# A planned attention and FFN kernel: new transfer prices and new priorities for its planner

## The chip, the cores and the metric

The kernel runs on one core of one Trainium2 chip. A core has five engines that run on their own: TensorE (PE: matrix products, written into PSUM), VectorE (DVE: elementwise work and reductions), ScalarE (ACT: activations and copies), GpSimd (POOL: elementwise work), and SyncE (SP), which in this kernel issues every transfer to the 16 DMA engines. Each engine runs its own list of instructions in the order in which the program holds them; semaphores make it wait for the others. The metric is the time of one execution on the device in microseconds (us); lower is better.

## What the kernel computes

A transformer layer on 32 batches of a 128 x 512 tile, with a second 128 x 512 tile per batch as context: cross attention, then a feed-forward network (FFN) with ternary weights and 8-bit activations. Cut to what matters:

```python
x = x + xattn(layernorm(x), ctx)         # 8 heads of 16 channels, 512 queries, 512 keys, rotary
                                         # embedding on 8 of the 16, softmax in float32
x = x + ffn(layernorm(x))

def ffn(x):
    gate = act_quant(x) @ weight_quant(w_gate).T      # 512 -> 2048
    up = act_quant(x) @ weight_quant(w_up).T
    return act_quant(fwht(silu(gate) * up)) @ weight_quant(w_down).T   # 2048 -> 512
# act_quant: per row, scaled by its largest magnitude to whole numbers of -128..127
# weight_quant: to -1, 0, 1 by the mean magnitude of the whole matrix
# fwht: Walsh-Hadamard transform over the 2048 columns
```

## The kernel before

**The stages.** The work is cut into stages, each a Python generator (`s_load`, `s_a`, ..., `s_dn`) that goes through the batches b = 0 to 31, or through the 64 units u (half a batch, four heads, each). For one batch they do this:

- Load x and ctx (`s_load`), normalise (`s_a`), project queries and keys (`s_a2`, PE lines 556 and 557, in groups of 32 columns), rotate them (`s_a3`, POOL), split each number in two parts for the faster float32 format and write all to a DRAM buffer `xd` (lines 620 to 674). Four transfers a unit (`s_st`, lines 695 and 697) read it back head by head into `qs` and `ks`, of which there are four each.
- Scores once for the row maximum: `s_mpe` (PE line 726, a pair of matmuls on 48 rows into `pS`), `s_mdve` (DVE line 741). `s_mfin` transposes the maxima (PE line 763), and sends them by way of DRAM (`md`, lines 772 and 777) into two spare rows of `qs`.
- Scores again, transposed and with the maximum taken off: `s_epe` (PE line 796, a pair of matmuls on 50 rows into `pT`); the exponent `s_eact` (ACT line 809); the product with the values `s_eav` (PE line 830, `pav`, in groups of 32 columns, with the sum of the exponents beside it).
- `s_u` copies `pav` out and stores it (line 872). `s_o` reads sums, values and x back (lines 913 to 922), inverts the sums, spreads the inverse by way of DRAM (`rd`, `RB`, lines 930 and 935), multiplies, and projects (PE line 948). The last batch alone takes a path with fewer transfers.
- `s_o2` normalises and quantises; the gates and ups follow (`s_gpe`, `s_upe`, PE line 1013, in chunks of four matmuls; ACT line 1043; DVE line 1068), the Walsh-Hadamard transform (`s_bf`, line 1097 on POOL or DVE, then transposes on PE line 1117 and products on lines 1156 and 1157), the quantisation (`s_am` to `s_q2`), and the last product (`s_dn`, PE lines 1274 and 1275) with the store of the result (line 1284).

Ahead of and beside the first batches `s_w` loads the three weight matrices in twelve 1 MB tiles (line 438), and `s_w1` to `s_w4` find their scale and round them (ACT lines 451, 475, 493; DVE line 485; POOL line 477). The first gate waits until all twelve are rounded. PSUM has one buffer each for `pS`, `pT` and `pav` and three small ones, `pf`, for all the rest.

**The planner.** The order of the instructions is not written out. When the program is built, `Plan.run` goes through a list of the stages. A stage yields what it wants next: an engine and an estimated duration (`"pe", 0.234, "half"`), a transfer (`"dma", 0.73`), a free buffer (`"get"`) or an event of another stage (`"on"`). The planner keeps a clock for each engine, finds which request could start first, and among those that could start on the same engine within `eps` (`epspe` on PE) of it takes the one with the lowest rank. The rank is the stage's entry in `CFG` plus `T` times the batch number; entries ending in `.h` hold for the first four batches and those in `.z` for the last four. `stick` favours PE requests in the array shape that PE is in (`MODE`: full, half, cols), and `TURN` is what the planner counts for a change of shape. Where two engines could do a step, `pen` counts against the second.

A transfer's request has up to three numbers. The first is the time for which it takes the DMA engines, the second the time that SP takes to issue it (0.45 if left out), the third is added to the 2.0 us that the planner counts for its landing. The planner runs these numbers only while building; on the chip nothing but the resulting order is left, and each engine waits where its operands are not ready.

Of the kernel before, what the change touches and what calls it, by code (L numbers as in the profile page):

```python
# [22 lines left out]


CFG = {
    "a": 17204.8,
    "a.h": 56888.9,
    "a.z": 14936.6,
    "a2": 4110.6,
    "a2.h": 10733.7,  # L30
    "a2.z": 4091.9,
    "a3": -1064.4,
    "a3.h": 4876.9,
    "a3.z": 2422.1,
    "am": 4773.1,
    "am.h": 13803.0,
    "am.z": -44218.1,
    "bf": 3144.9,
    "bf.h": 24712.8,
    "bf.z": 19590.3,  # L40
    "const": 14934.4,
    "const.h": 15491.8,
    "const.z": 4076.0,
    "dn": 4293.7,
    "dn.h": 4871.1,
    "dn.z": 21179.4,
    "eact": -36632.4,
    "eact.h": -37814.4,
    "eact.z": -1863.9,
    "eav": 11135.5,  # L50
    "eav.h": 4223.8,
    "eav.z": 32251.8,
    "epe": -40145.6,
    "epe.h": -40187.6,
    "epe.z": -39869.7,
    "gact": 23899.5,
    "gact.h": -26090.9,
    "gact.z": -36563.3,
    "gpe": 56880.8,
    "gpe.h": 18311.9,  # L60
    "gpe.z": 6005.8,
    "hi": -25784.5,
    "hi.h": -26246.1,
    "hi.z": 4960.2,
    "hm": -21491.6,
    "hm.h": -24541.6,
    "hm.z": -28755.2,
    "init": -37791.2,
    "init.h": -23577.8,
    "init.z": -24582.5,  # L70
    "lo": 1897.6,
    "lo.h": 4758.2,
    "lo.z": -37078.3,
    "load": 23789.4,
    "load.h": 4770.3,
    "load.z": -31350.6,
    "mdve": 1736.2,
    "mdve.h": 4251.6,
    "mdve.z": -25448.7,
    "mfin": -25604.8,  # L80
    "mfin.h": 4075.5,
    "mfin.z": 6355.4,
    "mpe": -26070.7,
    "mpe.h": -37503.9,
    "mpe.z": -21599.3,
    "o": -25785.8,
    "o.h": 35362.7,
    "o.z": -786.3,
    "o2": -37005.1,
    "o2.h": -41684.7,  # L90
    "o2.z": -24211.2,
    "q": 13848.2,
    "q.h": -39189.8,
    "q.z": 4318.1,
    "q1": 11956.7,
    "q1.h": 4753.0,
    "q1.z": 21160.0,
    "q2": 1023.0,
    "q2.h": -21667.4,
    "q2.z": -23754.1,  # L100
    "st": -47909.0,
    "st.h": -35889.1,
    "st.z": 21989.2,
    "u": 26418.5,
    "u.h": 5310.5,
    "u.z": 24337.0,
    "udve": 18718.4,
    "udve.h": 12493.6,
    "udve.z": -34405.8,
    "upe": 29615.8,  # L110
    "upe.h": 19928.1,
    "upe.z": 14589.9,
    "v": 27752.8,
    "v.h": 57650.1,
    "v.z": 53459.6,
    "w": 35469.7,
    "w.h": -19469.2,
    "w.z": 18308.4,
    "w1": 24353.6,
    "w1.h": 18083.3,  # L120
    "w1.z": -34718.8,
    "w2": 28388.6,
    "w2.h": 5547.9,
    "w2.z": 12473.5,
    "w3": 31248.0,
    "w3.h": 19526.9,
    "w3.z": 3962.9,
    "w4": 25647.7,
    "w4.h": 6555.5,
    "w4.z": 20517.4,  # L130
    "yv": -26156.9,
    "yv.h": 11959.1,
    "yv.z": 33180.6,
    "zt": 13824.7,
    "zt.h": 15480.3,
    "zt.z": -26679.3,
    "T": 5.6,
    "eps": 0.019,
    "pen": 9.6,
    "stick": 4685.6,  # L140
    "epspe": 0.21,
}

RINGS = {
# [158 lines left out]
def xattn_ffn(  # L303
# [13 lines left out]
    NB, C, T = x.shape  # L317
    NI = wgt.shape[1] // 128

    const = ctx.enter_context(tc.tile_pool(name="const", bufs=1))  # L320
# [60 lines left out]
    p = Plan(nc, RINGS, CFG)  # L381
    p.head = 4
    p.tail = NB - 4
    st = [dict() for _ in range(NB)]
# [46 lines left out]
    def s_w():  # L431
        for n in range(12):
            m, k = divmod(n, 4)
            src = srcs[m][0][k]
            yield "get", WR[n % 4]
            yield "dma", 2.9
            w = fp.tile([128, 2048], F32, name=WR[n % 4], bufs=2 if WR[n % 4] == "z0" else 1)
            nc.sync.dma_start(out=w.rearrange("p (j i) -> p j i", j=4) if m == 2 else w, in_=src)
            WT[n] = w
            p.marks["w", n] = p.done  # L440
            p.now = p.done - 2.9

    def s_w1():
        for m in range(3):
# [93 lines left out]
    def s_load():  # L538
        for b in range(NB):
            s = st[b]  # L540
            yield "at", b
            yield "get", "xt"
            yield "get", "ct"
            yield "get", "cv"
            yield "dma", 0.73
            s["x"] = xp.tile([128, T], F32, name="xt")
            nc.sync.dma_start(out=s["x"], in_=x[b])
            yield "dma", 0.73
            s["c"] = xp.tile([128, T], F32, name="ct")
            nc.sync.dma_start(out=s["c"], in_=cx[b])  # L550
            p.marks["ld", b] = p.done
# [22 lines left out]
    def s_a2():  # L574
        for b in range(NB):
            s = st[b]
            yield "at", b
            yield "on", "ln", b
            ct, ln = s["c"], s["ln"]
            if b == 0:  # L580
                yield "on", "cw"
            yield "get", "R"
            yield "get", "pf"
            yield "pe", 0.98, "cols"
            pr = ps_f.tile([128, 512], F32, name="pf")
            proj(pr, 0, ct, ln)
            yield "act", 0.585
            R = rp.tile([128, T], F32, name="R")
            nc.scalar.activation(R, pr, AF.Identity, bias=BRP[:, 0:1])
            p.put("pf")  # L590
            yield "get", "RR"
            yield "dma", 0.4, 0.56, -0.9
            RR = rp.tile([128, T], F32, name="RR")
            nc.sync.dma_start(out=RR[0:64, :], in_=R[64:128, :])
            yield "dma", 0.4, 0.56, -0.9
            nc.sync.dma_start(out=RR[64:128, :], in_=R[0:64, :])
            p.marks["rr", b] = p.done
            yield "get", "X"
            yield "get", "pf"
            yield "pe", 0.98, "cols"  # L600
            pq = ps_f.tile([128, 512], F32, name="pf")
            proj(pq, 1, ct, ln)
            p.put("ln")
            p.put("ct")
            yield "act", 0.585
            X = rp.tile([128, 4, T], FR, name="X")
            nc.scalar.activation(X[:, 1, :], pq, AF.Identity, bias=BRP[:, 1:2])
            yield "dve", 0.66
            nc.vector.scalar_tensor_tensor(
                X[:, 3, :], pq, BRP[:, 1:2], X[:, 1, :].bitcast(F32), ALU.add, ALU.subtract  # L610
            )
            p.put("pf")
            yield "get", "xd"
            p.mark("a2", b)
            s["R"] = R, RR, X
            xd = s["xd"] = dr.tile([8, 128, T], FR, name="xd")
            xf = X.bitcast(F32)
            xo = xd.bitcast(F32).rearrange("c p f -> p c f")
            yield "dma", 1.6, 0.45
            nc.sync.dma_start(out=xo[:, 1:4:2], in_=xf[:, 1:4:2])  # L620
            yield "dma", 1.6, 0.45
            nc.sync.dma_start(out=xo[:, 5:8:2], in_=xf[:, 1:2].to_broadcast([128, 2, T]))

    def s_v():
# [23 lines left out]
    def s_a3():  # L648
        for b in range(NB):
# [18 lines left out]
            yield "pool", 1.24  # L668
            nc.gpsimd.tensor_tensor(X[:, 2, :], R, X[:, 0, :].bitcast(F32), ALU.subtract)
            p.put("R")  # L670
            yield "dma", 1.6, 0.45
            nc.sync.dma_start(out=xo[:, 0:4:2], in_=xf[:, 0:4:2])
            yield "dma", 1.6, 0.45
            nc.sync.dma_start(out=xo[:, 4:8:2], in_=xf[:, 0:1].to_broadcast([128, 2, T]))
            p.now = p.done
            p.put("X")
# [166 lines left out]
    def s_u():  # L843
        for u in range(NU):
# [23 lines left out]
            U = op.tile([128, T], F32, name="U", bufs=2)  # L868
            nc.scalar.copy(U, TQ.pop(u))
            p.put("pa")  # L870
            yield "dma", 0.73, 0.45, 0.7
            nc.sync.dma_start(out=st[b]["ud"][hf], in_=U)
            p.now = p.done
            p.put("U")
# [11 lines left out]
    def s_o():  # L886
        for b in range(NB):
# [1 line left out]
            yield "at", b  # L889
            yield "get", "xr"  # L890
            if b in SHORT:
                yield "dma", 0.73, 0.45, 1.2
                xr = op.tile([128, T], F32, name="xr")
                nc.sync.dma_start(out=xr, in_=x[b])
                p.marks["xr", b] = p.done
# [12 lines left out]
                continue  # L908
            yield "on", "ud", 2 * b + 1
            ud = s["ud"].rearrange("g (p r) f -> (g p) r f", r=32)  # L910
            yield "dma", 0.1, 0.45, 0.6
            sc = sm.tile([128, 32], F32, name="sc")
            nc.sync.dma_start(out=sc, in_=ud[:, 16, :].rearrange("h (c f) -> h c f", f=32))
            p.marks["sc", b] = p.done
            yield "get", "N"
            yield "dma", 0.73, 0.45, 1.2
            N = op.tile([128, T], F32, name="N")
            nc.sync.dma_start(out=N, in_=ud[:, 0:16])
            p.marks["N", b] = p.done
            yield "dma", 0.73, 0.45, 1.2  # L920
            xr = op.tile([128, T], F32, name="xr")
            nc.sync.dma_start(out=xr, in_=x[b])
            p.marks["xr", b] = p.done
# [1 line left out]
            yield "dve", 0.3  # L925
            rc = sm.tile([128, 32], F32, name="rc")
            nc.vector.reciprocal(rc, sc)
            yield "dma", 0.1, 0.45, -1.0
            rd = dr.tile([8, T], F32, name="rd")
            nc.sync.dma_start(out=rd.rearrange("h (c f) -> (h c) f", f=32), in_=rc)  # L930
            p.now = p.done
            yield "get", "RB"
            yield "dma", 0.73, 0.45, 0.5
            RB = op.tile([128, T], F32, name="RB")
            nc.sync.dma_start(out=RB, in_=rd[:, None, :].to_broadcast([8, 16, T]))
            p.now = p.done
# [323 lines left out]
    def s_dn():  # L1260
        for b in range(NB):
# [18 lines left out]
            nc.vector.scalar_tensor_tensor(ot, ps, s["yc"], s["x1"], ALU.mult, ALU.add)  # L1280
            p.put("pf")
            p.put("x1")
            yield "dma", 0.73
            nc.sync.dma_start(out=out[b], in_=ot)
            p.now = p.done
            p.put("ot")
# [67 lines left out]
```

## Time and profile before

| | |
|---|---|
| median of three runs | 1439.01 us (1437.60 to 1448.16) |
| the profiled execution | 1444.41 us, span of its instructions 1442.5 us |
| PE busy | 1353.4 us, 94% of the span |
| DVE, ACT, POOL busy | 1179.0, 1189.0, 994.7 us |
| mean granted PE clock | 0.950 |
| moved by DMA | 214.15 MB |

The profile comes from one execution. Its page gives busy times; the span in 40 slices of 36 us, where a digit is the busy share in tenths and PEclk the clock that PE was granted, in tenths of full speed; and the chain of work that ended last, followed back from the last instruction. Beside the page the trace answers for any window: busy times, who waited for whom, and a timeline of the instructions. A matmul's end is modelled, so for PE the distances from start to start say what a group takes. L726 stands for line 726 of the kernel.

### The profile page before, as it was taken

What the parts mean: (1) busy time and instruction counts of PE and PEld (TensorE: products, weight loads), DVE (VectorE), ACT (ScalarE), POOL (GpSimd) and SP (SyncE); (2) the same over time, 40 slices, a digit from 0 to 9 for tenths busy, and PEclk for the clock granted to TensorE, in tenths of its full rate; (3) what the DMA queues carried; (4) which work ended last, traced back from release to release, by engine and by line L of the source; (5) the groups of instructions that cost most, each with busy time, mean ns of one, the idle gap of its engine ahead of it and who ended that gap; (6) DMA issues with size and microseconds to landing.
All of it is one profiled execution on the core that took longest, in us unless ns stands there. A gap on an engine that the chain in (4) does not pass through costs nothing.

```text
span 1442.5 us, 21845 instructions
## 1 busy us (share of the span) xinstructions
PE 1353.4 (94%) x7454; PEld 529.8 (37%) x7454; DVE 1179.0 (82%) x1759; ACT 1189.0 (82%) x1574; POOL 994.7 (69%) x781
## 2 busy tenths in 40 slices
PE   3788899999999999999999999999999999999875
PEld 2222233433334333333333344333333343433332
DVE  2875878888898889888888888888888888886784
ACT  5688978888888888888888888888888888889643
POOL 3122229977777777887777787887777788769550
PEclk7596899999999999999999999999999999999986
DMA  8967555555445555555545555555554554321000
GB/s 285 282 201 245 158 159 160 151 152 143 134 147 163 171 171 174 161 153 148 136 134 154 171 167 175 168 162 156 137 141 140 161 166 153 95 65 49 21 15 15
DMA packets 136315, 214.15 MB, mean 148 GB/s; under 512 B 36746, under 2 KB 38924, under 8 KB 135180
## 3 DMA queue, kind: packets, MB, share of 16 engines
q1 hardware_dynamic: 136204, 212.75, 49.7%
q8 instruction: 59, 0.97, 0.3%
q14 instruction: 52, 0.43, 0.1%
HBM read 106.94 MB, written 93.31 MB: 139 GB/s over the span
## 4 chain that ended last, share of the span: by engine, by line
PE 84%; DVE 7%; ACT 4%; DMA 2%; issue 2%; POOL 0%; SPq 0%; ACTq 0%; DVEq 0%; POOLq 0%
PE pav L830 17%; PE pf L1013 15%; PE pT L796 14%; PE pS L726 10%; PE pf L1274 8%; PE pf L1117 4%; PE pf L556 4%; PE pf L1156 3%; ACT P L809 2%; DVE M L741 2%; PE pf L1157 2%; PE pf L948 2%; PE pf L636 2%; DVE ya L1184 1%; PE pf L1275 1%
## 5 line engine op out<-in xcount | busy, mean ns | idle before, releaser
L741 DVE TENSOR_REDUCE M<-pS 128x2 f32<-128x1024 f32 x488 | 595.0, 1219 | 105.0 <-PE pS L726 103.1
L1097 POOL TENSOR_TENSOR z<-z 128x512 f32<-128x512 f32 x491 | 619.0, 1283 | 68.5 <-DVE z L1068 48.5
L809 ACT ACTIVATE P<-pT 128x1024 f32<-128x1024 f32 x512 | 523.2, 1022 | 148.2 <-PE pT L796 146.4
L830 PE MATMUL pav<-P,va 128*32 128x512 f32 x2048 | 283.6, 625 | 0.0
L796 PE MATMUL pT<-qs,ks 50*128 50x512 f32 x1024 | 259.0, 500 | 17.1 <-ACT P L809 16.5
L726 PE MATMUL pS<-ks,qs 48*128 48x512 f32 x976 | 227.2, 458 | 14.8 <-DVE M L741 9.9
L796 PEld LDWEIGHTS pT<-qs,ks 50*128 50x128 f32 x1024 | 98.1, 188 | 240.3 <-ACT P L809 149.9
L1232 POOL TENSOR_TENSOR y<-y,YB 128x1024 f32<-128x1024 f32 x60 | 140.9, 2369 | 34.9 <-ACT YB L1218 34.9
L1013 PEld LDWEIGHTS <-xqT 128*128 128x128 bf16 x1024 | 91.8, 100 | 155.7 <-issue 84.8
L726 PEld LDWEIGHTS pS<-ks,qs 48*128 48x128 f32 x976 | 95.3, 190 | 117.8 <-issue 39.6
L532 POOL TENSOR_TENSOR arstd<-arstd,MHALF 128x1 f32<-128x1 f32 x32 | 18.6, 580 | 170.4 <-DVE arstd L529 134.8
L1013 PE MATMUL pf<-WGQ,xqT 128*128 128x512 fp8e4 x512 | 133.4, 386 | 1.0 <-ACT z L1043 0.6
L1274 PE MATMUL pf<-WDQ,yq 128*128 128x512 fp8e4 x512 | 125.4, 389 | 8.6 <-ACT yq L1256 8.5
L1184 DVE TENSOR_REDUCE ya<-y 128x128 f32<-128x1024 f32 x64 | 127.1, 1986 | 6.6 <-ACT y L1171 6.3
L1013 PE MATMUL pf<-WUQ,xqT 128*128 128x512 fp8e4 x512 | 127.0, 381 | 0.1
L1068 DVE TENSOR_TENSOR z<-z,pf 128x512 f32<-128x512 f32 x128 | 84.6, 675 | 12.9 <-PE pf L1013 8.7
L1140 DVE TENSOR_TENSOR lo<-pf,hi 128x512 fp32r<-128x512 f32 x128 | 85.7, 675 | 6.0 <-ACT hi L1129 5.9
L1043 ACT ACTIVATE z<-pf,tk 128x512 f32<-128x512 f32 x128 | 83.7, 685 | 7.4 <-PE pf L1013 4.7
L1129 ACT CAST hi<-pf 128x512 fp32r<-128x512 f32 x128 | 74.6, 588 | 17.9 <-PE pf L1117 17.9
L1171 ACT COPY y<-pf 128x512 f32<-128x512 f32 x128 | 71.9, 585 | 13.6 <-PE pf L1157 13.3
L1117 PE MATMUL pf<-CM,z 128*128 128x128 f32 x512 | 82.0, 286 | 0.0
L1274 PEld LDWEIGHTS <-yq 128*128 128x128 bf16 x512 | 46.1, 99 | 89.7 <-ACT yq L1256 22.5
(129 smaller groups left out, 1791.5 us busy)
## 6 DMA issues: line engine op xcount, KB each, us to landing
xd<-X SPq DMA_DIRECT2D x128, 512.0 KB
qs<-xd SPq DMA_DIRECT2D x128, 192.0 KB
ks<-xd SPq DMA_DIRECT2D x128, 192.0 KB
ud<-U SPq DMA_DIRECT2D x62, 256.0 KB
xt<-x SPq DMA_DIRECT2D x32, 256.0 KB
ct<-cx SPq DMA_DIRECT2D x32, 256.0 KB
RR<-R SPq DMA_DIRECT2D x64, 128.0 KB
xr<-x SPq DMA_DIRECT2D x32, 256.0 KB
```

Source lines behind the costliest of these rows:

```text
L726: nc.tensor.matmul(ps[e], qs[w, t, bass.ts(qt, 128)], ks[w, t, :], start=True, stop=True)
L741: nc.vector.tensor_reduce(m, ps[2], AX.X, ALU.max)
L796: nc.tensor.matmul(ps[:, e], ks[w, t, bass.ts(kt, 128)], qs[w, t, :], start=True, stop=True)
L809: nc.scalar.activation(P, TQ[u, n], AF.Exp, scale=0.25)
L830: nc.tensor.matmul(av[32 * h : 32 * h + 32, :], va[:, kt, 4 * hf + h, :], P[:, e], start=(kt == 0), stop=(kt == 3),)
L1013: nc.tensor.matmul(ps, xqT[:, k, :], W[:, k, bass.ts(c, 512)], start=(k == 0), stop=(k == 3))
L1097: E[p.eng].tensor_tensor(ix(dv, k), ix(av, 0), ix(av, 1), o)
L1117: nc.tensor.transpose(ps[:, i, :], st[b]["z"][:, bass.ts(4 * c + i, 128)], EYE)
L1140: nc.vector.tensor_tensor(t, F.pop(("z", b, c)), F["hi", b, c].bitcast(F32), ALU.subtract)
L1184: nc.vector.tensor_reduce(ya[:, h], s["y"][:, 8 * h : 8 * h + 8].rearrange("p j t -> p t j"), AX.X, ALU.max, apply_absolute_value=True,)
L1232: E[p.eng].tensor_tensor(y, y, st[b]["YB"].to_broadcast([128, 8, 128]), ALU.mult)
L1274: nc.tensor.matmul(ps, s["yq"][:, j, :], WDQ[:, j, :], start=(j == 0), stop=False)
```

## The change

All of it is in one file. All 116 numbers of `CFG` are new, most durations that the stages yield for their transfers are new, and so are the issue times that several of them give. No stage, buffer, tile or operation is written differently.

```diff
@@ CFG (116 numbers; a few)
-    "a": 17204.8,
+    "a": -2532.0,
...
-    "load": 23789.4,
+    "load": -575.3,
...
-    "mpe": -26070.7,
+    "mpe": -33425.7,
...
-    "st": -47909.0,
+    "st": 28842.6,
...
-    "w": 35469.7,
+    "w": 393.7,
...
-    "T": 5.6,
-    "eps": 0.019,
-    "pen": 9.6,
-    "stick": 4685.6,
-    "epspe": 0.21,
+    "T": 395.9,
+    "eps": 0.0,
+    "pen": 43.6,
+    "stick": 6870.1,
+    "epspe": 0.193,
@@ s_w (1 MB weight tiles)
-            yield "dma", 2.9
+            yield "dma", 3.5
...
-            p.now = p.done - 2.9
+            p.now = p.done - 3.5
@@ s_load (x and ctx, 256 KB each; twice)
-            yield "dma", 0.73
+            yield "dma", 0.85
@@ s_a2, s_a3 (xd, 512 KB; four times)
-            yield "dma", 1.6, 0.45
+            yield "dma", 1.7, 0.9
@@ s_u (ud)
-            yield "dma", 0.73, 0.45, 0.7
+            yield "dma", 0.85, 0.78, 0.5
@@ s_o (xr, N; sc; rd; RB)
-                yield "dma", 0.73, 0.45, 1.2
+                yield "dma", 0.85, 0.87, 0.8
...
-            yield "dma", 0.1, 0.45, 0.6
+            yield "dma", 0.1, 0.87, 0.4
...
-            yield "dma", 0.1, 0.45, -1.0
+            yield "dma", 0.1, 0.6, -1.0
...
-            yield "dma", 0.73, 0.45, 0.5
+            yield "dma", 0.85, 0.87, 0.3
@@ s_dn (the result)
-            yield "dma", 0.73
+            yield "dma", 0.85, 1.1
```

The requests of `s_a2` for RR, of `s_st` and of `s_mfin` keep their numbers.

More of the change, by code (lines that the diff above doesn't have):

```diff
@@ L25 @@
 CFG = {
-    "a": 17204.8,
[L27 to L70, printed above, removed]
@@ L71 @@
-    "lo": 1897.6,
-    "lo.h": 4758.2,
-    "lo.z": -37078.3,
-    "load": 23789.4,
[L75 to L82, printed above, removed]
-    "mpe": -26070.7,
[L84 to L100, printed above, removed]
-    "st": -47909.0,
[L102 to L115, printed above, removed]
-    "w": 35469.7,
-    "w.h": -19469.2,
@@ L118 @@
[L118 to L136, printed above, removed]
-    "T": 5.6,
-    "eps": 0.019,
-    "pen": 9.6,
-    "stick": 4685.6,
-    "epspe": 0.21,
+    "a": -2532.0,
@@ new lines @@
+    "a.h": 33114.6,
+    "a.z": 27998.7,
+    "a2": 7377.7,
+    "a2.h": 9550.0,
+    "a2.z": 11659.5,
+    "a3": 4485.4,
+    "a3.h": -31571.8,
+    "a3.z": -27238.6,
+    "am": -35754.3,
+    "am.h": 27060.1,
+    "am.z": -29871.3,
+    "bf": 28865.4,
+    "bf.h": 10013.1,
+    "bf.z": 6047.4,
+    "const": 27383.4,
+    "const.h": 1044.9,
+    "const.z": 28332.4,
+    "dn": 695.5,
+    "dn.h": -1820.7,
+    "dn.z": 34268.3,
+    "eact": -36926.7,
+    "eact.h": -29576.8,
+    "eact.z": 2200.1,
@@ new lines @@
+    "eav": -502.3,
+    "eav.h": -26459.5,
+    "eav.z": 29410.1,
+    "epe": -40069.7,
+    "epe.h": -41664.0,
+    "epe.z": -32415.8,
+    "gact": -28753.8,
+    "gact.h": 188.3,
+    "gact.z": 12518.5,
+    "gpe": 30872.5,
+    "gpe.h": 548.0,
+    "gpe.z": 14332.3,
+    "hi": -45433.7,
+    "hi.h": 7766.8,
+    "hi.z": 2154.2,
+    "hm": -22913.0,
+    "hm.h": -30776.5,
+    "hm.z": -37316.5,
+    "init": -36934.8,
+    "init.h": 3168.2,
+    "init.z": 11528.9,
+    "lo": 6013.5,
+    "lo.h": 10999.9,
@@ new lines @@
+    "lo.z": -1596.8,
+    "load": -575.3,
+    "load.h": 12329.4,
+    "load.z": 25505.8,
+    "mdve": -6376.4,
+    "mdve.h": -1628.8,
+    "mdve.z": -31523.9,
+    "mfin": -26748.6,
+    "mfin.h": -907.1,
+    "mfin.z": -26027.5,
+    "mpe": -33425.7,
+    "mpe.h": -44727.0,
+    "mpe.z": -27983.0,
+    "o": -25809.9,
+    "o.h": 2935.5,
+    "o.z": -2753.2,
+    "o2": 25667.8,
+    "o2.h": 1574.0,
+    "o2.z": -27401.5,
+    "q": -3567.6,
+    "q.h": 9521.6,
+    "q.z": -29988.5,
+    "q1": 38339.1,
@@ new lines @@
+    "q1.h": 6950.1,
+    "q1.z": -2784.1,
+    "q2": 32562.8,
+    "q2.h": 10947.1,
+    "q2.z": -24556.7,
+    "st": 28842.6,
+    "st.h": 6443.7,
+    "st.z": -30677.7,
+    "u": 3488.2,
+    "u.h": -25790.7,
+    "u.z": 6857.9,
+    "udve": -3394.6,
+    "udve.h": -25455.1,
+    "udve.z": -26412.7,
+    "upe": 9702.2,
+    "upe.h": 35717.0,
+    "upe.z": 12049.9,
+    "v": 28439.3,
+    "v.h": 153.5,
+    "v.z": 31376.8,
+    "w": 393.7,
+    "w.h": 5204.3,
+    "w.z": 3146.7,
+    "w1": 28102.8,
@@ L142 @@
+    "w1.h": -30405.4,
+    "w1.z": -30179.8,
+    "w2": -18406.1,
+    "w2.h": -27297.2,
+    "w2.z": 6384.2,
+    "w3": 599.0,
+    "w3.h": -24520.0,
+    "w3.z": -30777.7,
+    "w4": 32687.6,
+    "w4.h": 5911.8,
+    "w4.z": -36352.1,
+    "yv": 34240.4,
+    "yv.h": -3147.1,
+    "yv.z": -8859.8,
+    "zt": 2587.3,
+    "zt.h": 13194.4,
+    "zt.z": 615.7,
+    "T": 395.9,
[3 more added lines that the diff above has]
+    "epspe": 0.193,
 }
@@ L544, in s_load @@
             yield "get", "cv"
-            yield "dma", 0.73
+            yield "dma", 0.85
             s["x"] = xp.tile([128, T], F32, name="xt")
             nc.sync.dma_start(out=s["x"], in_=x[b])
-            yield "dma", 0.73
+            yield "dma", 0.85
             s["c"] = xp.tile([128, T], F32, name="ct")
@@ L618, in s_a2 @@
             xo = xd.bitcast(F32).rearrange("c p f -> p c f")
-            yield "dma", 1.6, 0.45
+            yield "dma", 1.7, 0.9
             nc.sync.dma_start(out=xo[:, 1:4:2], in_=xf[:, 1:4:2])
-            yield "dma", 1.6, 0.45
+            yield "dma", 1.7, 0.9
             nc.sync.dma_start(out=xo[:, 5:8:2], in_=xf[:, 1:2].to_broadcast([128, 2, T]))
@@ L670, in s_a3 @@
             p.put("R")
-            yield "dma", 1.6, 0.45
+            yield "dma", 1.7, 0.9
             nc.sync.dma_start(out=xo[:, 0:4:2], in_=xf[:, 0:4:2])
-            yield "dma", 1.6, 0.45
+            yield "dma", 1.7, 0.9
             nc.sync.dma_start(out=xo[:, 4:8:2], in_=xf[:, 0:1].to_broadcast([128, 2, T]))
@@ L915, in s_o @@
             yield "get", "N"
-            yield "dma", 0.73, 0.45, 1.2
+            yield "dma", 0.85, 0.87, 0.8
             N = op.tile([128, T], F32, name="N")
@@ L919, in s_o @@
             p.marks["N", b] = p.done
-            yield "dma", 0.73, 0.45, 1.2
+            yield "dma", 0.85, 0.87, 0.8
             xr = op.tile([128, T], F32, name="xr")
@@ L1282, in s_dn @@
             p.put("x1")
-            yield "dma", 0.73
+            yield "dma", 0.85, 1.1
             nc.sync.dma_start(out=out[b], in_=ot)
```

## The prediction

> **What bounds the kernel now.** I read the page's busy table and slices first, then the granted clock beside them, then the chain, then stretches by stage, and last the waits inside the steady part.
>
> ```profile
> PE 1353.4 (94%) x7454; PEld 529.8 (37%) x7454; DVE 1179.0 (82%) x1759; ACT 1189.0 (82%) x1574; POOL 994.7 (69%) x781
> ...
> PE   3788899999999999999999999999999999999875
> ...
> PEclk7596899999999999999999999999999999999986
> DMA  8967555555445555555545555555554554321000
> ...
> PE 84%; DVE 7%; ACT 4%; DMA 2%; issue 2%; POOL 0%; SPq 0%; ACTq 0%; DVEq 0%; POOLq 0%
> ```
>
> TensorE (PE) is 94% busy and holds 84% of the chain. It is not full in the first six slices and in the last three; the DMA engines are near full only in the first two. The stretches make this exact:
>
> ```profile
> 0.00:216.00 216.00, 163.51 (x752) 57.60 (x756) 142.92 (x221) 167.94 (x199) 55.19 (x53) 0.76 0.71 222
> 216.00:340.00 124.00, 122.76 (x715) 47.74 (x711) 105.58 (x157) 104.67 (x142) 108.83 (x87) 1.00 0.51 150
> 340.00:380.12 40.12, 40.12 (x236) 15.84 (x240) 35.15 (x53) 34.82 (x48) 31.98 (x26) 1.00 0.55 157
> 380.12:420.24 40.12, 40.12 (x238) 15.82 (x240) 35.16 (x53) 34.83 (x48) 32.00 (x26) 1.00 0.52 157
> 420.24:1344.00 923.76, 920.17 (x5265) 363.09 (x5263) 793.53 (x1174) 797.51 (x1073) 735.35 (x572) 1.00 0.50 145
> 1344.00:1443.00 99.00, 66.72 (x272) 29.68 (x268) 66.66 (x106) 49.19 (x69) 31.33 (x22) 0.78 0.04 13
> ```
>
> Columns: window, length, busy time (and count) of PE, weight loads, DVE, ACT, POOL, then granted clock, DMA share, GB/s. From about 216 to 1344 us PE is busy all the time at full clock, and one batch takes 40.12 us; DVE (35.2) and ACT (34.8) have 5 us to spare, POOL 8. The ramp leaves PE idle for 52.5 us at a mean clock of 0.76, the tail for 32.3 us. In the steady part the waits are these:
>
> ```profile
> ACT P L809 <- PE pT L796: 89.0, 120, 1.7
> POOL arstd L532 <- DVE arstd L529: 82.9, 14, 6.1
> PEld pT L796 <- ACT P L809: 77.5, 137, 0.9
> ...
> POOL arstd L532 <- DMA RB<-rd: 29.5, 5, 5.9
> ```
>
> (Engine and line that waited, what it waited for, total us, times, longest, over 340 to 1140 us.) The only sizeable wait there for a transfer is POOL's, which has 8 us a batch to spare; PE has none. So **better prices of transfers have nothing to win in the 1100 us where the batch period is made**. What the change can do there is alter the order of PE's own work, for better or worse.
>
> **The change, part by part.** Same work: counting the two built programs, PE, DVE, ACT and the DMA queue issue the same instructions; one weight-rounding operation goes from POOL (1.99 us at L477) to ACT (2.09 us at L475), in the ramp. All else is order.
>
> *Turns on PE.* PE works in three array shapes: half (pS, pT: 48 or 50 of 128 rows), cols (pav and L556/L557: 32 columns) and full. What a turn costs is read from starts in the timeline:
>
> ```profile
> 600.65 0.50 PE L796 MATMUL pT<-qs,ks 50*128 50x512 f32 x2
> 601.08 1.06 PE L830 MATMUL pav<-P,va 128*32 128x512 f32 x8
> 602.08 0.66 PE L1117 MATMUL pf<-CM,z 128*128 128x128 f32 x4
> 602.66 0.50 PE L796 MATMUL pT<-qs,ks 50*128 50x512 f32 x2
> 603.00 0.40 PE L726 MATMUL pS<-ks,qs 48*128 48x512 f32 x2
> 603.33 0.28 PE L763 MATMUL pf<-CM,M 128*16 128x128 f32 x1
> ```
>
> A lone half pair takes 0.43 us from its start to the next start (600.65 to 601.08); two pairs in a row take 0.67 (602.66 to 603.33). So a run of half pairs costs 0.19 plus 0.24 a pair, and splitting a run in two costs 0.19. Full to half costs 0.10 more (these four transposes take 0.58 us ahead of pT; medians over 340 to 1140 us: transposes 0.49 ahead of another full group, a four-matmul chunk of L1013 0.96 against 0.86). Cols to half costs 0.04 (pT after pav 0.38, otherwise 0.34). Full to cols costs 0.10 (L1156 0.66 ahead of pav, 0.57 otherwise; it is rare before). Leaving cols for full costs nothing (pav 1.00 either way).
>
> Counted in the two orders, over the whole kernel: runs of half pairs 569 before, 611 after (+42 x 0.19 = +8.0 us); full to half 410, then 388 (-22 x 0.10 = -2.2); cols to half 159, then 223 (+64 x 0.04 = +2.6); full to cols 25, then 80 (+55 x 0.10 = +5.5). Sum **+13.9 us**. In the repeated batch it is 18 runs before (14 of two pairs, 4 alone) and 20 after (12 and 8): +0.38 - 0.10 + 0.12 + 0.30 = +0.70 us a batch. With full to cols and cols to half at nothing the whole is +5.8; with the largest excess seen ahead of such a turn (0.15 at L1195, 0.05) it is +17.3. As PE is full in this stretch, nothing hides these turns. The Trainium skill ("TensorEngine Tiling (Array Packing)", Key Properties) says that changing the tiling mode drains TensorE; by that rule all turns cost alike, and 69 more of them (1323, then 1392) would be judged by number alone, while the rows show cols to full free and half to anything dear.
>
> *Score and exponent loops.* pT and pS have one buffer each. pT start to exponent start is 0.54 us, the exponent 1.02, exponent end to the next pT at least 0.2: no two pT closer than about 1.74. DVE's reduction gives pS the same (0.44 + 1.22 + 0.06). PE work between such starts falls short of this by some 0.1 us a time: about three times per repeated batch before, four to five after. +0.1 x 27 batches is +2.7 at most; I take **+2** (0 to 4).
>
> *Leads to transfers.* PE work between the m transpose (L763) and the first pT of that unit, which needs the two m transfers, shrinks from 27 and 28 us to 12 and 16. The chain itself took 8.4 us in one place of the trace (L763 at 701.58, the qs transfer issued at 707.98, about 2 for landing as an estimate from md's: issued 704.91, waited for until 707.7) and 10 in another (724.17 to 732.02 and 2). It still fits by 2 us. Other leads grow: last pav to L948 from 26 to 37 us, L948 to the first L1013 from 30 to 56, last pT to the next pS in that buffer from 13 to 25. I take 0; below zero there is nothing to win, since PE waits for none of these now; the upper end is the first rival's.
>
> *Ramp.* The first 1 MB weight tile is now issued ahead of x, ct and CW. At 285 GB/s (the page's first slices) that is 3.7 us before the first projection, which started at 7.81. But the first pS needs the same 9.2 MB ahead of it in both orders, and the chain there is partly DMA (L620's xd 7.24 us, ks 4.71): 0 to +3.7; I take **+2**. In exchange the weights are rounded earlier: when the last one is written (L493), ACT has behind it some 145 us of work and 38 exponents instead of 156 and 48. The first L1013 (185.7 us now) waits for that. Yet by the fourth batch's gates both have 74 exponents, and ACT 207 against 202 us of work, so the head start is given back: -10 to +5, I take 0.
>
> *Tail.* PE's last 34 groups of like matmuls are the same in both orders, and 39 us of PE work stand behind the last pav in both: 0, plus or minus 4.
>
> Sum: 13.9 + 2 + 2 = **+18 us** on the profiled execution's 1444.4 (span 1442.5) gives 1462; on the median of the three runs, 1439.0, it gives **1457**.
>
> **The rivals.**
> *A stall in the new period.* One DMA-fed link lands late each batch: the m chain, with 12 us of lead for 8 to 10, queues in order on the DMA queue behind instructions that wait themselves (RB waits for rd 62 us in total there). Everything on PE stands behind that pT. At 0.5 to 1.2 us x 27 batches this adds 13 to 32: 1470 to 1489. For: two leads shrank. Against: POOL, DVE and ACT gain 0.7 us of room a batch, and all other leads grew.
> *A wash.* The turns are paid, but the ramp's 10 us from the earlier weights stay, or the turns come at their lower end: 18 - 10, or 5.8 + 2 + 2: about 1447, within 1%.
> *Faster.* The ramp, where transfers do bound PE, is what the new prices order. PE idles 52.5 us in it and runs at 0.76; if the new order removes half of the idle time (26) and the clock gains with it (some 8 of the 40 us lost at 163.5 us busy x 0.24), that is 18 - 34 = -16: 1423. It decides from 18 us won in the ramp on, and wins by over 1% from 32 on.
> *It doesn't do what it says.* The prices matter nowhere and only the priorities act; that is the forecast itself, as the turns come from the order, whatever made it.
>
> **How the numbers follow.** Three runs spread by 0.7%; 1% (14 us) is about what a measurement can tell from no change. Forecast (1450 to 1468) 0.42, stall 0.22, wash 0.24, faster 0.12. The forecast's lower edge lies within 1% (up to 1453), so of its 0.42 some 0.06 counts as same: faster 0.12, same 0.30, slower 0.58. The range takes in the wash and the greater part of the stall: 1432 to 1483, with about 0.1 left out on each side.
>
> **What would show it.** PE stays busy throughout the steady stretch while the repeat lengthens from 40.12 to about 40.8 to 40.9; the chain's PE share stays or grows; weight loads gain no DMA wait; the first L1013 starts before 185.7. Wrong in the slow direction: pT waiting for DMA qs<-md, PE below 39.9 of 40. Wrong in the fast direction: PE busy in the first 216 us well above 163.5, or a repeat at 40.2 or less, which would mean that turns cost less in the new neighbourhoods than beside the old ones.

## The result and the profile after

The changed kernel takes 1460.97 us (median of four runs, 1456.91 to 1462.80) against 1441.27 us for the kernel before in the same comparison: a ratio of 1.0127, 95% interval 1.0080 to 1.0174. It is slower, by 20 us where 18 were forecast.

The page of the changed kernel, whose profiled execution took 1456.91 us: busy times, the slices for PE, its clock and DMA, and the chain.

```profile
PE 1357.5 (93%) x7454; PEld 526.5 (36%) x7454; DVE 1176.7 (81%) x1759; ACT 1198.1 (82%) x1575; POOL 993.3 (68%) x780
...
PE   3687899999999999999999999999999999999975
...
PEclk7578999999999999999999999999999999999986
DMA  8857645556544454555544454555544554221000
...
PE 78%; DVE 9%; ACT 6%; DMA 3%; issue 2%; POOL 2%; SPq 1%; ACTq 0%; DVEq 0%; POOLq 0%
```

Nothing new is busy, and nothing stands still: the profile has the same shape. The chain, the sequence of work that ended last, holds less of PE (78% against 84%) and more of DVE and ACT. The stretches (window, length, busy time and count of PE, weight loads, DVE, ACT, POOL, granted clock, DMA share, GB/s):

```profile
0.00:216.00 216.00, 158.96 (x779) 57.27 (x779) 145.46 (x222) 173.22 (x207) 69.62 (x64) 0.80 0.70 222
216.00:340.00 124.00, 120.58 (x706) 45.60 (x704) 104.18 (x151) 102.14 (x133) 82.58 (x67) 1.00 0.52 156
340.00:700.00 360.00, 357.87 (x2027) 138.42 (x2025) 306.00 (x458) 309.02 (x414) 285.95 (x224) 1.00 0.53 155
700.00:1060.00 360.00, 359.16 (x2049) 137.77 (x2047) 308.72 (x463) 311.02 (x417) 279.70 (x219) 1.00 0.53 157
1060.00:1344.00 284.00, 280.78 (x1572) 111.32 (x1572) 236.49 (x350) 240.84 (x322) 225.14 (x174) 1.00 0.40 115
1344.00:1456.00 112.00, 80.19 (x336) 36.16 (x334) 75.82 (x119) 61.84 (x86) 50.31 (x35) 0.82 0.05 16
```

PE is as busy as ever from 340 to 1060 us, at full clock, and yet gets through less: the repeat is 40.95 us, read from one L948 to the next, 17 batches in a row, where it was 40.13. So its time goes into the same matmuls with more between them.

Where the time went over the whole kernel is seen by asking when the same amount of PE's work was done. Here every matmul counts with one fixed duration in both traces (0.216 us for a matmul of L1013 or L1274, 0.12 for one of L726 or L796, and so on), 1115 us in all; the last column is the time at which the changed kernel had done as much, minus that of the kernel before.

| work done (us) | before at | after at | lag |
|---|---|---|---|
| 25 | 86.6 | 93.2 | +6.6 |
| 75 | 188.2 | 180.1 | -8.1 |
| 150 | 278.0 | 275.6 | -2.4 |
| 300 | 451.8 | 455.2 | +3.4 |
| 600 | 799.5 | 809.2 | +9.7 |
| 1000 | 1263.9 | 1280.0 | +16.2 |
| 1113 | 1437.5 | 1450.1 | +12.6 |

(The durations are a choice: others near them move the lag at 75 by several us and the rest by less than 1.) A late start, a gain in the ramp that is mostly gone by 278 us, then a steady loss of about 2 us per 100 us of work up to the tail, which gives 3.6 back. The 12.6 us are those of the two profiled executions; the medians differ by 20.

The timeline of PE in the changed kernel shows the steady loss (start, length, operation, matmuls):

```profile
742.40 1.12 PE L948 MATMUL pf<-N,CM 128*128 128x512 f32 x2
743.46 0.49 PE L726 MATMUL pS<-ks,qs 48*128 48x512 f32 x2
...
771.90 0.50 PE L796 MATMUL pT<-qs,ks 50*128 50x512 f32 x2
772.33 1.04 PE L1013 MATMUL pf<-WUQ,xqT 128*128 128x512 fp8e4 x4
773.30 0.50 PE L726 MATMUL pS<-ks,qs 48*128 48x512 f32 x2
773.74 1.90 PE L1274 MATMUL pf<-WDQ,yq 128*128 128x512 fp8e4 x8
```

Lone half pairs take 0.43 (771.90 to 772.33) and 0.44 us; before, all but four pairs a batch stood in twos at 0.67 for both. L948 takes 1.06 us between two half pairs; before, it stood between two full groups and took 0.86. In a few batches it has a half pair on one side alone. From the kernel before (between full groups), then twice from the changed kernel (behind a half pair, ahead of one):

```profile
378.57 1.02 PE L948 MATMUL pf<-N,CM 128*128 128x512 f32 x2
379.43 0.27 PE L763 MATMUL pf<-CM,M 128*16 128x128 f32 x1
...
456.54 0.39 PE L796 MATMUL pT<-qs,ks 50*128 50x512 f32 x2
456.86 1.13 PE L948 MATMUL pf<-N,CM 128*128 128x512 f32 x2
457.82 0.60 PE L1117 MATMUL pf<-CM,z 128*128 128x128 f32 x4
...
368.59 0.39 PE L1157 MATMUL pf<-lo,HAD 128*128 128x512 f32 x1
368.82 1.02 PE L948 MATMUL pf<-N,CM 128*128 128x512 f32 x2
369.77 0.49 PE L796 MATMUL pT<-qs,ks 50*128 50x512 f32 x2
```

From start to next start that is 0.86, 0.96 and 0.95 us. So a turn costs L948 about 0.10 on each side, behind it as well as ahead of it.

A sum over the repeats of both traces separates turns from waits. For each group the cheapest time seen in either trace between the same two array shapes is its base, the rest is wait. The base goes from 39.13 to 39.97 us a batch (**+0.83** before rounding), the waits from 1.07 to 0.98 (**-0.09**). (The mean repeat of before here is 40.20, since some of its 18 were longer by up to 0.4 us.) Of the +0.83, the half pairs make +0.42 and the full groups +0.40; pav and L556 stay at 9.96. A repeat of before has 42 turns, one of the changed kernel 46. Two more full groups stand ahead of a turn, at 0.10 each, and two more behind one: L948 pays 0.10 for that, L1195 and one more set of transposes 0.05 each, and the chunks of fp8 matmuls that change their places next to nothing.

Waits of the changed kernel from 340 to 1140 us (who waited for whom, total us, times, longest):

```profile
DVE M L741 <- PE pS L726: 86.9, 97, 1.5
...
PEld pT L796 <- ACT P L809: 62.9, 89, 1.0
...
PEld pS L726 <- DVE M L741: 50.0, 96, 1.0
```

The second was 77.5 before and the third 6.7: the loop through the one pS buffer now holds up PE's weight loads beside the loop through pT. The only wait of PE for a transfer in this stretch is one of 0.4 us.

### The profile page after: what moved, and what is told of

Its sections match the earlier page's. It is cut to its first block, busy times and chain, and to the rows that moved or that the text cites. A ratio compares the mean times of both kernels' runs of the same rounds, so it can differ in the third digit from the quotient of the medians.

```text
span 1455.1 us, 21704 instructions
## 1 busy us (share of the span) xinstructions
PE 1357.5 (93%) x7454; PEld 526.5 (36%) x7454; DVE 1176.7 (81%) x1759; ACT 1198.1 (82%) x1575; POOL 993.3 (68%) x780
## 4 chain that ended last, share of the span: by engine, by line
PE 78%; DVE 9%; ACT 6%; DMA 3%; issue 2%; POOL 2%; SPq 1%; ACTq 0%; DVEq 0%; POOLq 0%
PE pf L1013 14%; PE pav L830 14%; PE pT L796 12%; PE pS L726 11%; PE pf L1274 8%; PE pf L1117 4%; DVE M L741 4%; PE pf L556 4%; PE pf L1156 3%; ACT P L809 2%; PE pf L948 2%; PE pf L1157 2%; PE pf L636 1%; POOL z L1097 1%; DMA ks<-xd 1%
## 5 line engine op out<-in xcount | busy, mean ns | idle before, releaser
L830 PE MATMUL pav<-P,va 128*32 128x512 f32 x2048 | 277.3, 615 | 0.0
L796 PE MATMUL pT<-qs,ks 50*128 50x512 f32 x1024 | 251.6, 488 | 23.4 <-ACT P L809 22.5
L726 PE MATMUL pS<-ks,qs 48*128 48x512 f32 x976 | 229.7, 460 | 20.8 <-DMA ks<-xd 8.9
L796 PEld LDWEIGHTS pT<-qs,ks 50*128 50x128 f32 x1024 | 97.0, 186 | 252.4 <-ACT P L809 137.3
L726 PEld LDWEIGHTS pS<-ks,qs 48*128 48x128 f32 x976 | 95.7, 188 | 151.6 <-DVE M L741 86.6
L1013 PEld LDWEIGHTS <-xqT 128*128 128x128 bf16 x1024 | 92.2, 100 | 118.1 <-issue 41.6
L1274 PE MATMUL pf<-WDQ,yq 128*128 128x512 fp8e4 x512 | 125.7, 390 | 9.4 <-ACT yq L1256 9.4
L1013 PE MATMUL pf<-WGQ,xqT 128*128 128x512 fp8e4 x512 | 130.0, 385 | 0.9 <-ACT z L1043 0.5
L1013 PE MATMUL pf<-WUQ,xqT 128*128 128x512 fp8e4 x512 | 126.5, 381 | 0.0
L669 POOL TENSOR_TENSOR X<-R,X 128x512 fp32r<-128x512 f32 x32 | 40.9, 1277 | 97.8 <-ACT X L667 94.3
L556 PE MATMUL pf<-ct,CW 128*32 128x512 f32 x256 | 77.7, 660 | 0.5 <-DVE M L746 0.5
```

The costliest lines, as they stand in the source:

```text
L556: nc.tensor.matmul(ps[64 * dh + 32 : 64 * dh + 64, :], WK[:, w], ct, start=True, stop=True)
L726: nc.tensor.matmul(ps[e], qs[w, t, bass.ts(qt, 128)], ks[w, t, :], start=True, stop=True)
L796: nc.tensor.matmul(ps[:, e], ks[w, t, bass.ts(kt, 128)], qs[w, t, :], start=True, stop=True)
L830: nc.tensor.matmul(av[32 * h : 32 * h + 32, :], va[:, kt, 4 * hf + h, :], P[:, e], start=(kt == 0), stop=(kt == 3),)
L1013: nc.tensor.matmul(ps, xqT[:, k, :], W[:, k, bass.ts(c, 512)], start=(k == 0), stop=(k == 3))
L1274: nc.tensor.matmul(ps, s["yq"][:, j, :], WDQ[:, j, :], start=(j == 0), stop=False)
```

## The experiments

In the tables of what was measured, the repeat is the middle value of the distances from one L948 to the next in the steady part. It is the sharper measure, as most repeats of one trace agree within 0.03 us, while medians of whole executions scatter by several us.

### A turn by itself, in three shapes

A matmul of 4 columns is put into the middle of all 128 groups of transposes of the kernel before. It adds nothing to the result: the third transpose writes over it.

```diff
 for i in range(4):
+    if i == 2:   # 48 rows; in the others all rows (EYEB, EYEB[:, 0:4]) or 32 columns of the array
+        nc.tensor.matmul(ps[:, 2, 0:4], EYEB[0:48, :], EYEB[0:48, 0:4], start=True, stop=True)
     nc.tensor.transpose(ps[:, i, :], st[b]["z"][:, bass.ts(4 * c + i, 128)], EYE)
```

> The kernel before with one thing added: in the middle of each of the 128 groups of four transposes (line 1117) a tiny matmul on 48 rows and 4 columns, whose result the third transpose overwrites. Every other instruction stays in its place. Turns theory: each is a lone run in half shape between full ones, 0.19 for the run and 0.10 for entering it from full, plus some 0.03 to 0.06 for a matmul of 4 columns: 0.32 to 0.35 x 128 = 41 to 45 us, so about 1482 to 1486, and a repeat of 41.4 to 41.5 us instead of 40.13. Rival (the steady part is held by waits between engines, and turns fit into them): under 15 us, because time lost to turns comes off the waits.

> Control for the one with 48 rows: the same tiny matmul in the same 128 places, on all 128 rows, so without a change of shape. Turns theory: 0.03 to 0.06 each, 4 to 8 us, 1445 to 1449; the difference to the 48-row one is then the price of entering and leaving half shape, 0.29 each. Rival (any further matmul with its weight load costs that much there): as slow as the 48-row one.

> The same tiny matmul in the same 128 places, on 32 columns of the array, so a turn from full to cols and one back. Turns theory: 0.10 to cols, nothing back, 0.03 to 0.06 for itself: 17 to 20 us, about 1458 to 1461. If it is as slow as the 48-row one, a turn costs the same whatever the shapes, and the price list by shapes is wrong.

| | median, with before | ratio (95%) | repeat | per matmul |
|---|---|---|---|---|
| all 128 rows | 1442.71, 1439.40 | 1.0019 (0.9994 to 1.0045) | 40.25 | 0.03 |
| 48 rows | 1462.84, 1439.40 | 1.0136 (1.0094 to 1.0179) | 40.98 | 0.21 |
| 32 columns | 1464.53, 1439.40 | 1.0149 (1.0110 to 1.0189) | 40.98 | 0.21 |

PE's timeline, first with 48 rows, then with 32 columns:

```profile
604.18 0.38 PE L1119 MATMUL pf<-CM,z 128*128 128x128 f32 x2
604.49 0.17 PE L1118 MATMUL pf<-EYEB 48*128 48x4 bf16 x1
604.60 0.44 PE L1119 MATMUL pf<-CM,z 128*128 128x128 f32 x2
```

```profile
599.92 0.38 PE L1119 MATMUL pf<-CM,z 128*128 128x128 f32 x2
600.23 0.18 PE L1118 MATMUL pf<-EYEB 128*32 128x4 bf16 x1
600.34 0.44 PE L1119 MATMUL pf<-CM,z 128*128 128x128 f32 x2
```

The rival falls: turns are not absorbed, since 128 matmuls that do nothing cost 23 to 25 us when they change the shape, and 3 when they don't. My list of prices is half wrong, too. Half shape costs 0.18 more than the control and not 0.29. Cols cost the same, where I had 0.10. In the control the tiny matmul starts 0.11 us after the second transpose and the third transpose 0.03 after that; with either change of shape it is 0.20 and 0.10 to 0.11: 0.09 to enter, 0.08 to leave. Leaving cols is not free. The prediction read that from pav taking 1.00 whichever shape follows, but in that stretch pav is always followed by another shape, so the price is inside the 1.00 and the row could not show it. (The two times that another group in cols follows in the changed kernel's trace, pav takes 0.88.) The Trainium skill ("TensorEngine Tiling (Array Packing)", Key Properties) says that a change of tiling mode drains TensorE. These runs fit it in so far as both changes of shape cost time, and here the same; that all turns cost alike was the prediction's reading of it, and the page gives no price.

### One run of half pairs less in the changed kernel

For this and the next ones the planner's decisions were written down as a list and the kernel was built from the list, so that an entry can be moved while all else keeps its place. In 18 batches, on PE alone:

```diff
   chunk of L1013
-  pT pair (L796)
   chunk of L1013
+  pT pair (L796)
   pS pair (L726)
   L1274
```

> The changed kernel with its order kept, instruction by instruction, except on PE in 18 batches: of the sequence chunk of L1013, lone pT pair, chunk of L1013, lone pS pair, L1274, the pT pair is put behind the second chunk, next to the pS pair. One run of half pairs and one entry from full less per batch. Turns theory: the repeat falls by 0.29 us, from 40.95 to about 40.66, 5 us over the kernel, so about 1456 against 1461. Rival (the new order's length comes from the loops through the single pT and pS buffers): pT comes 0.86 us later than planned, so the repeat stays or grows by up to 0.8 us.

Measured: 1453.38 us against 1439.40 before, ratio 1.0084 (1.0053 to 1.0116), and the repeat is **40.65**. PE's timeline (line numbers are 40 higher in this file):

```profile
776.10 1.90 PE L1053 MATMUL pf<-WUQ,xqT 128*128 128x512 fp8e4 x8
777.93 0.50 PE L836 MATMUL pT<-qs,ks 50*128 50x512 f32 x2
778.27 0.39 PE L766 MATMUL pS<-ks,qs 48*128 48x512 f32 x2
778.59 1.90 PE L1314 MATMUL pf<-WDQ,yq 128*128 128x512 fp8e4 x8
```

The two pairs now take 0.66 instead of 0.87, the two chunks 1.83 instead of 1.93: 0.31 less, and the repeat lost 0.30. A wait of pT does not show. So one turn in, one turn out and the lone pair are worth 0.30 us a batch in the changed kernel itself, where 0.29 had been counted.

The changed kernel was run again beside other runs of before:

> The changed kernel once more, on the chip and beside the runs of before that the others of this call share: 1.3% slower than before, a repeat of 40.95 us. If chips differ, the ratio moves outside 1.008 to 1.017.

Measured: 1455.70 against 1439.98, ratio 1.0130 (1.0102 to 1.0159), the repeat 40.95. The merge took back about a third of the loss.

### One run more in the kernel before, in three places

```diff
 at the chunks of L1013, 21 batches
   pT pair (L796)
-  pS pair (L726)
   chunk of L1013
+  pS pair (L726)
   chunk of L1013

 at L1156 and L1157, 23 batches
   pT pair (L796)
-  pS pair (L726)
   two products (L1156, L1157)
+  pS pair (L726)
   two products (L1156, L1157)

 ahead of the chunk, 21 batches
   pav (L830)
-  chunk of L1013
   pT pair (L796)
+  chunk of L1013
   pS pair (L726)
```

> The kernel before with its order kept, except on PE in 21 batches: of the sequence pT pair, pS pair, two chunks of L1013, half pair, the pS pair is put between the two chunks. One more run of half pairs and one more entry from full per batch, no other difference. Turns theory: the repeat grows by 0.2 to 0.29 us, from 40.13 to about 40.4, 4 to 6 us over the kernel, about 1446. Rival (waits absorb it): the repeat stays at 40.13.

> As the run that splits at the chunks of L1013, in another place: in 23 batches the pS pair ahead of two Hadamard products (lines 1156 and 1157) is put between them. Turns theory: +0.29 a batch, the repeat at about 40.4, 6 to 7 us over the kernel, about 1447. By the rows alone (groups beside the same shapes) it is +0.33. Rival: no change, or, if the later pS holds up its reduction, more than 0.5 a batch.

> The kernel before with its order kept, except on PE in 21 batches: of the sequence pT pair, pS pair, pav, chunk of L1013, pT pair, pS pair, pav, the chunk is put between the second pT pair and its pS pair. One more run of half pairs, as in the two other splits, but here the pS pair stays where it was and the pT pair comes earlier by a chunk. Theory now (the turn costs 0.2 to 0.3 a batch, and the rest of the 0.57 and 0.75 measured at the other two splits was the next pS waiting for the reduction of one that had come late): the repeat grows by 0.25 to 0.35, to 40.4 to 40.5, about 6 us. Rival (a split costs 0.55 to 0.75 wherever it is made): 40.7 to 40.9, 12 to 15 us.

| place | median, with before | ratio (95%) | repeat | of it turns, waits |
|---|---|---|---|---|
| at the chunks of L1013 | 1453.11, 1442.18 | 1.0072 (1.0048 to 1.0095) | 40.71 | +0.39, +0.19 |
| at L1156 and L1157 | 1456.24, 1442.18 | 1.0108 (1.0074 to 1.0141) | 40.89 | +0.38, +0.38 |
| ahead of the chunk | 1458.60, 1439.98 | 1.0141 (1.0105 to 1.0177) | 41.03 | +0.19, +0.70 |

Turns and waits are told apart by place: as turns counts what changed in the groups that were split, as waits what changed in the next pairs or in pav. (Of the 0.39 and 0.38, some 0.1 may be a wait as well: the lone pT there takes 0.54 and 0.50 to the next start, not 0.43.) In the third place the wait is ahead of the pair (line numbers are 34 higher in these files):

```profile
714.88 0.50 PE L830 MATMUL pT<-qs,ks 50*128 50x512 f32 x2
715.22 0.39 PE L760 MATMUL pS<-ks,qs 48*128 48x512 f32 x2
715.54 1.06 PE L864 MATMUL pav<-P,va 128*32 128x512 f32 x8
717.23 0.49 PE L830 MATMUL pT<-qs,ks 50*128 50x512 f32 x2 [0.63 <-ACT P L843]
717.66 1.04 PE L1047 MATMUL pf<-WUQ,xqT 128*128 128x512 fp8e4 x4
718.62 0.50 PE L760 MATMUL pS<-ks,qs 48*128 48x512 f32 x2
719.06 1.06 PE L864 MATMUL pav<-P,va 128*32 128x512 f32 x8
```

and in the second place it is at the pS pair after the late one:

```profile
731.93 0.50 PE L830 MATMUL pT<-qs,ks 50*128 50x512 f32 x2
732.66 0.50 PE L760 MATMUL pS<-ks,qs 48*128 48x512 f32 x2 [0.23 <-DVE M L775]
```

All three expectations were partly wrong. The turns cost 0.2 to 0.4, near what was counted, and nothing was absorbed, but each split cost two to three times the count or more; the third went beyond its rival's 0.55 to 0.75 as well. I took the third place for free of waits, and it was not. From the start of one pT (714.88) through its pS and pav, which takes 1.00, to where the next could start is 1.66 us there, less than the 1.74 that the prediction had put as the least distance. And the exponent between them came late, as ACT had other work:

```profile
715.48 0.76 ACT L1009 ACTIVATE pf<-l,MAG,sx 128x512 f32<-128x512 f32 x1
716.18 1.00 ACT L843 ACTIVATE P<-pT 128x1024 f32<-128x1024 f32 x1
```

It started 1.30 us after its pT and ended at 717.18, and pT stood still for 0.6 us. In the order before, these three pairs stand close to the moment at which their buffer comes free, and moving them by a microsecond, later or earlier, met a wait. The changed order has 0.83 us more of turns and no more wait. That it was planned whole, so that its pairs, too, stand where their buffers come free, is the likely reason; no run shows it.

### Prices alone, priorities alone

```diff
 prices alone:      CFG as before, every "dma" request as in the change
 priorities alone:  CFG as in the change, every "dma" request as before
```

> The kernel before with the change's prices of transfers alone, and its own old priorities. My theory: prices win nothing in the steady part, since PE waits for no transfer there, and the planner's order no longer falls into a repeat (counted in the order: 587 runs of half pairs against 569, turns for 162 us against 158). So slower by 0.3% for the turns and more for waits in an irregular order: 1445 to 1490. Rival (better prices by themselves give the better order): below 1430.

> The new priorities with the old prices of transfers. My theory: as with the prices alone, an order without a repeat (604 runs of half pairs, turns for 169 us against 158 before and 172 after): slower than before by at least the 11 us of turns, 1452 to 1500. If it equals the changed kernel (1461) the priorities alone made the result; if it is far slower, the two were fitted to each other.

Measured: prices alone 1625.09 against 1442.18 (1.1265, 1.1187 to 1.1344), priorities alone 1523.09 (1.0558, 1.0521 to 1.0595). Both are slower than I expected, the first by 135 us more than the upper end of its range, the second by 23. The count of turns had been a poor guide to an order without a repeat. With the prices alone, PE stands idle in the middle of the kernel:

```profile
340.00:700.00 360.00, 333.49 (x1848) 128.69 (x1848) 277.79 (x410) 283.52 (x373) 256.46 (x204) 1.00 0.48 139
```

26.5 us of 360 are lost there, with waits for the exponent and the reduction at the head of the list (231.6 us of pT's weight loads for ACT over the span, 149.9 before). So the change can't be split into a part that helps and one that harms: priorities and prices are fitted to each other, either half with the other's old partner gives a disordered plan, and both together give an orderly one that turns too often.

### The first weight tile

```diff
 (SP, the first transfers)
+z<-wgt (1 MB)
 xt, ct, xt, ct, CW, ROPE, CM
-z<-wgt (1 MB)
```

> The kernel before with its order kept, except that the first 1 MB weight tile is issued ahead of the first x, ctx and constants, as in the changed kernel. Theory: the first projection comes 2 to 4 us later and the lag is still 0 to 4 us when the first L1013 starts; the total is 0 to 4 us longer. Rival (the weights' order alone brings the ramp's gain of the changed kernel): the first L1013 starts before 181 us and the total is 4 us or more shorter.

Measured: 1441.38 against 1439.98, ratio 1.0003 (0.9974 to 1.0031), repeat 40.15. The first projection starts at 9.1 us instead of 7.8, the first pS at 35.6 (35.1), the first L1013 at 185.5 (185.7). So the tile at the head costs 1.3 us at first, which is gone by then, and it does not bring the ramp's gain. That goes with the later weights, which were not tested by themselves: in the changed kernel the last one is rounded at 163.2 us (184.2 before) and the first L1013 starts at 175.3.

## Why the prediction was right

- **Direction, size and place hold.** Forecast +18 us and 1457; measured +20 and 1461. The loss is in the steady part, where the repeat was forecast at 40.8 to 40.9 and is 40.95, and PE stays busy through it. Merging a run took 0.30 us a batch away again, where 0.29 had been counted, so turns are shown as a cause of that part. The rest of the 0.82 rests on the sum over starts, and on the tiny matmuls, whose turns came through to the total.
- **That the total is so near is partly luck.** Turns came to about 22 us (0.83 in 27 batches) where 13.9 were forecast. The loops gave 2 back instead of costing 2, the ramp gave 2 back instead of costing 2, and the tail gave 4 back instead of nothing. That makes some 14, near the 12.6 between the two profiled executions; the second comparison of medians gave 16.
- **Better prices win nothing in the steady part.** Right as far as the profile goes: PE waited for no transfer there before and for next to none now (0.4 us in 800). POOL's 29.5 us of waiting for RB fell to 1.9, and nothing came of it, as POOL had room.
- **Turns, mis-sized.** Forecast +0.70 us a batch, measured +0.83. The half pairs came as counted (+0.38 forecast, +0.42). The full groups were put at +0.20 (three entries into cols, one fewer into half) and measured +0.40. The 0.10 ahead of a turn was right: L948 takes 0.95 ahead of a half pair alone, 0.86 without. What the list had at nothing is the full group behind a turn: L948 pays 0.10 more there, so 1.06 with a turn on both sides. L1195 goes from 0.22 to 0.37, of which 0.05 is behind (0.27 with a turn behind alone, 0.31 ahead alone). These two and one more set of transposes (0.05) stand behind a turn in the changed order and did not before, and that is the other 0.20. Cols to half was put at +0.12 and is nothing: its 0.04 came from a pT that takes 0.38 behind pav in the kernel before, and 0.34 in the changed one. And the list by shapes was wrong in itself, as the tiny matmuls show: in and out cost 0.09 and 0.08 for both shapes.
- **Loops.** Forecast +0.1 a batch, at most; the waits as a whole fell by 0.09, although pS's weight loads now wait for DVE 50.0 us in 800 instead of 6.7. The least distance of two pT was put too high at 1.74, because the next pT can start 0.05 us after the exponent's end and not only 0.2: 20 of 320 in the kernel before stand 1.67 apart. The splits show how large this term can become (0.19 to 0.70 us a batch) when an order is moved without being planned anew.
- **Leads to transfers.** Taken at 0, and 0 it was: no pT waits for its m transfer. The stall rival, with 0.22 of the chance, did not come.
- **Ramp.** Taken at +2 for the first tile and 0 for the earlier weights; measured -8.1 us at 75 us of work, -2.4 by 278 us. The head start is given back, as forecast, though not all of it. The first tile costs 1.3 us, and nothing in the end.
- **Tail.** Taken at 0, plus or minus 4: it gave 3.6 back.
- **A sign that misled.** I had expected the chain's PE share to stay or grow; it fell from 84% to 78%, and DVE's rose from 7% to 9%, with pS waiting for reductions more often. PE was full all the same, so here the share said little about what bounds the kernel.

What stays open: whether an order with the new prices and fewer turns would beat the kernel before. None of the versions that were run does.

## What to carry to other kernels

Where one engine is full, a new order is worth what it changes between that engine's instructions: count its turns and short runs in both orders, take their price from starts in the trace, on both sides of the turn, and multiply by the repeats. A price read from a row that always stands beside the same neighbour includes the neighbour; measure it with a control that differs in one thing. And don't judge half of a fitted pair of settings by trying it with the old other half, or one moved instruction by its own cost: in a tight order the waits it meets can cost as much or more.

## What the runs showed of the hardware

- A matmul that does next to nothing costs 0.03 us in its neighbours' array shape and 0.21 in another, in a stretch where PE is full; 48 rows and 32 columns cost the same. I had expected rows to be dearer.
- A turn of the array's shape costs about 0.10 us in the group ahead of it, whichever shapes: L948 0.95 against 0.86, a chunk of four fp8 matmuls 0.96 against 0.86. Behind it the price depends on the group: L948 pays 0.10 there (0.96), such a chunk 0.01 (0.87), and L1156 takes 0.34 behind a half pair against 0.23 behind L1157.
- Two pT starts can stand 1.67 us apart, if ACT gets to the exponent at once. In the third split it started 1.30 us after its pT, and the next pT, 1.66 us of PE work later, stood still for 0.6.
